# Four graph layers over 32 batches: score rows through a line in DRAM, statistics for pairs of batches, and work moved between VectorE, ScalarE and GpSimd

## The chip, the core and the metric

The kernel runs on one core of a Trainium2 chip. The metric is the device time of one execution in microseconds; a median over several executions is given. A profile of one execution shows, for each engine, every instruction with its start and end: PE (TensorE matmul, with PEld for its weight loads), DVE (VectorE), ACT (ScalarE), POOL (GpSimd) and SP (SyncE, which issues the DMAs here). Each engine works off its instructions in the order in which they stand in its own queue, and waits at an instruction whose inputs are not there yet.

## What is computed

The input x has 32 batches of 512 nodes with 128 features, in float32; adj is one 512 x 512 matrix of zeros and ones for all batches. Four layers follow one another, each in the frame `x = layernorm(x + layer(x))`, where the outer layernorm has no weights:

```python
# layer 0
e = (x @ a_i)[:, :, None] + (x @ a_j)[:, None, :]
mean, var = over all of e of one batch
e = leaky((e - mean) * rsqrt(var + 1e-14) * adj + adj)
h = sigmoid(einsum('bij,bjd->bid', softmax(e, axis=1), x))
# layer 1: h = x @ Wp + bp; masked softmax over leaky(s_src + s_dst), times adj, @ h
h_gat = relu(layernorm(..., gat_g, gat_b))
z = ((1 + eps) * h_gat + adj @ h_gat) @ W1 + b1
z = relu(layernorm(z, mlp_g, mlp_b))
h = relu(z @ W2 + b2 + h_gat)
# layer 2: A is a softmax over masked values; M the unit matrix
h = (A * M) @ (x @ W[0]) + (A * (1 - M)) @ (x @ W[1]) + bias
# layer 3: h = x @ W; masked softmax over leaky(e_src + e_dst), @ h, then elu
```

In layers 1 and 3 a score is the sum of one number of the row's node and one of the column's node. The column's numbers must therefore stand as a row of 512 on every partition.

## The kernel before

A batch is a tile of 128 partitions by 4 blocks by 128 features: node 128c + p is row p of block c. Constants (masks, the transposed adjacency, the matrix of layer 2, weights) are made once by `prepare_l1`, `prepare_l2` and `prepare_l3`. Then a loop over the batches (L1046) calls `layer0` to `layer3`. These functions do not issue anything: a recorder (L267) notes every operation, with what it reads and writes. At the end `order` (L335) gives them out one by one. Which of the operations that are ready comes next is read from a packed string, ORDER, which holds a complete order for all engines, worked out ahead; many batches are in flight at once. While it gives them out, `order` assigns tiles to 70 buffers of 128 x 512 in SBUF, to 110 small ones, and to the 8 PSUM banks, and where its own clock shows a gap on PE of over 250 ns and a bank is free, it puts transposes named `warm` into it (`fill`, L381). All operations are issued by one helper line, L418, so the profile is read by tile names.

Names end in the layer: `_r` layer 0, `_g` layer 1, `_t` layer 2, `_a` layer 3. A name with `p_` in front lies in a PSUM bank.

- `layer0` (L843). For the first five batches (FIRST) PE makes the two scores n of every node; from then on DVE does, with eight multiply-and-sum operations (xa_r). `rows_of` turns the scores into a row. The mean and the variance over all pairs come from two products with the matrix `share` (p_m_r, p_v_r) and tiny operations on DVE; two powers on POOL give r and its inverse sd. The three wide passes over e_r (DVE once, ACT twice) follow for each of four blocks, then the product p_o_r. After tanh on ACT, POOL makes y = 0.5 y + 0.5 and adds x, and DVE normalises (x_r).
- `rows_of` (L807) spreads a column over the partitions with four transposes on PE into a bank.
- `masked_softmax` (L817), for layers 1 and 3: the row from `rows_of` (p_d_g, p_d_a); four DVE operations add the mask and take the maximum (e_g, e_a, mx); two ACT passes follow.
- `layer1` (L916). After the product p_o_g the normalisation of hg has, in turn: four DVE operations with mean and reciprocal deviation, two POOL passes with gat_g and gat_b, a relu on DVE, and a POOL pass for hb. The product p_g_g needs hg.
- `layer2` (L975). POOL multiplies x by the diagonal of A (xd_t); PE transposes that; ACT copies it to dt_t.
- `layer3` (L1000). After the product p_o_a, elu is made of two ACT passes (ex_a), one POOL pass (exp - 1) and a DVE operation with the maximum; the result is normalised on ACT (x_a) and stored.
- `layer_norm` (L781) makes the statistics on DVE (st, mv), adds epsilon on POOL (ve, L761), takes the power -1/2 on POOL (rs, L756), and normalises on ACT with `normalise` (L766, which first makes sh on DVE) or on DVE with `normalise_dve` (L775).

Of the kernel before, what the change touches and what calls it, by code (L numbers as in the profile page):

```python
# [17 lines left out]
P = 128  # L18
# [10 lines left out]
WARM = 12  # L29
SMALLS = 110  # L30
BUFFERS = 70

# [4 lines left out]
c-mch$C4~Nk{tqCYY{55>b_>TaWRWA<AVSHXFRyGV`gPkiV%Rq{RkkeWLmI;bM_K?QzE{n5dRk9KSGH3FFb_T|N6&0<M%(m-yivVck;aapU+#_!`So7-  # L37
u1Biz6rq}e{c5rkoS|WL>{6}LXPVogpq5lMe-VVKF{ks|M%zld_LFvkgvlVHsrY`yYM)BIEB1a6er_!9&<T1`>zXUf1~rQ&|)uJ4>L^4B<ZR}P%#RbGm
&kr|CMA`L&^VYwuScJ%eLPBPiy~o;(utPx7H3)njRxhJ91B>m)@*wX*D~oZMMc3bKH+)V%-n(cU!qBrO3>a*smCzv)nl+9p~9`#strm1?HlQ(cuivCBn
Ed&IE%8ezC0KC}tfyjOnI4EaY(7&baWLMQV?O(UcC0hcWwazuB8;xCz`l9G3~vQETn?HW6&9CLSMk@H&JLXUO%TwuY;YY^wLVMX#wbS{JVmg*MZ81ZRk  # L40
phpZAudaaZqhnHDcX|*xZsG#NkuZeb2DXqN1nUqr`JEE;}C7Gesk<%fvm!j5WywKWUH&s(wvNwUVR-+cqA9NPpL~qd2WR%21c&mgF*+l7O5XK|~${81p
G9E$m*_enYzLj1Jt%y*<W#MXaQn=_<_Qa;_j4rX~8a&3Vq!>*K)&=94(YRy|7)X7TRJ5iVA3K8HyiGdWR8qqjn^tSDwINves^iK&c%K`drI}b-)uE(Zb
swSWqN@+B#<tU=9MzQJO>j9Fl6pkM6NVONurX)tTFbetoYQD0a<Cy0kJj)hWrNR_uIX_aQ|Hc<T&SUe(%M;FCOk+Pihi)mTn!;)DP18@AJNqnKhfjy^>
?_Q>pHG<o#|Ls&np~9IgS)&upxzJ9a=fklnC<*O1k8Pkf8+;N+3oQpMy)ux9oZ;Bp~9+5r<48hV1myIUwUKMzLWV(+D|-q#qk@bE`|7;^g7BTq~=LRwB
qAc@2e|*c!fc+=zga@|2U)xs)tK5Q0mM6yZunB2X7@cgOMMdEwlnlmzp5I))7o4k_a#+s(;;YXa$Ft+zF!Iz~pUi$CqD7jlJ1ry09B<IE;oaL^PP(bGC
3Ls3{=pl*<_s7os7K_yXwa!yea#33D>;=}^C2t|ny)HbTy;&;WVD~v{*SX#z4=ZbTFNUDy=BoWjTdbsW+ZNd73CX1ZJ6~iuMrvJ8EnO)mjX%r;VntR1O
7n~V^y1;k1mXbnCMr_3BAa1A{?7z=J2)-eeBdKyZIGV_ggXDaqL<3@^38koCbpT0}IMj}=;u6gjl!*;Os3}U3Vh8@vx8uOR1{uaQGY3@^#g8hc65)`V>
BCuJqKX(p0~nAP3`LzZ@(7GlWr0<PvS#B6>OLyvQZZ>`XVpy<v^oP10XeAdY*3ZxvkpiSr<i3{3kwk4<Bs4M>iq@=l(%!$C0T$@(x;U1d-<CS9MA=<rH
7ABw3I{w)@YS<#Q5bpOD1M<1dAdbo{DN6<$yn5bTp`Uqmw5k+6;s!mLiHKBwk!*E%TDZky#cjBCM>k7)h<U0UW9lJK$N!mIdErlT*)3G^UDDP4P-tudG
#~kThL%LAVlJ9|92;2f|1*DTE{v@W(v|X)r`JBKa_EET|x7)uoqOR4lRO*khF?c!V5r8-SG#tV%$RTx3xxqwS1EMp3~`0OMG|pfVqL<URuayhDN>M-1#  # L50
hNtx`yQN~8V5}?gEolFwCg5{62TZZN_!b!q8Gg2pIKs1#VXofdkdL-0^%p;OKm5955KZi`6Bq?Sg3Byp6MEuiv%2S!;R#@jMGY<5mcW;`~RjRD<3g~?z
%A?f0=Sb=pl0{<5!vWz5N>3y6l-1rI-05Q%Y?Uku;71_H@}P1&QXyG}ERk<f){>|W#4A*-l|Hh}vpGUn3Alr#QOE{?05Dum;+#}CiNe)*FRj>LqQt4Ux
Gn`V876E(81j+Z6uu?jU5yC4Te)-7Z66dv0**zRrId6yyb?_oAZv#%K!s79AYzYL%;vF5kI0V@($NCrk=fM{YCC+jeu8g$26YFEOgLnem(*aOx=wSNse
P#?HT{?10n}OhB;6iy36a5qPc}o5AYFs%wSmwC5~y3>dXB{wzy_-L2-q|Tr-_bZydp|k@4|F|Uhsj7GE%_%oM9AX{82MFbu)R*l)AkSu9hgBNi0C+;=r
~Q>~-|(%tt?u74lelfE!XxzD!gOU#*G^;!$hKRqrTo8U1}Oyb>rXA9L(}qnxX#q1HGN&9qQ;8q9IFr<In^79)D)bm*ho1QJf*63~n>Dk%^{G!8nW#+nN
RKt^^HaIb`nE6Jh(I*K{&dFBE3&38TP{UlP`Pfe?wrNxoYQBv<+v2idG7gCZ$LOfb>^*PUp3*R6c%b#2cPwpamgQq@^-C!lsX50&X@*mGTprZcZSTl-8
KL8=@@D0V*MLRl(uV#)A`^qZBgmxt(oltjPM<5T-G&Wv2uLfjzOu36l+Cj}BZ8^XahXNHxD<hEB{^iqJW%8(lUh$y=KVlvo+|!CLWtFOW%4?lzt%P?K@
O9>tECwt!H3K=jeUn4Zcvr!r#kqb5ca;l?c49QIk`bsf0_wi>|4B1k7i9yVAdy&76)BB?dWAB{+!xXVk*-?kh~SqH!;CGmw#tHd4iHE&f$dQ(NKcTf=M
a+MBA`GxEJ(;625JvG7;UAp!!Bhy(6njCi_V9}lhxr^v!z*hf?kdeb%#zs1D2wh>R=AGb)hW8q%Ozc$euapxLO-(&W6(~bEC{2*)M*o`+lGMycYi`Y}U
Fy55M30WAFR>8vA4IHJ*?87&Gjrf6V(_<~grxjQO2rj8FglUVZ$m@$K(9pV3DhSKWG!hEBpusUeWMmmxk?PsZH`*_p99L!2c}5h03u9T+2%Gh(Ijjm<(  # L60
YGt+gM(>r_B3s7^~u)u4vdw<l*b~%~MbR$r5c({Rp&n~xjfta1GbvHm!6)ngFreOe*OKnB9Qozd)3tlD3s*F(kZkLag2tBACAPG?jZ{Zk}t%s+mheXn$
&?{hp<N=@nCl+KO9xZm&BKQF1KQQ8Z+;QbLD?gqGc+tmwU!ueAiQ0NSZ?OJ*!d{KDw_4;WX9-ZR;g9?R_kOheY3;YY?FJ&;?K0-a9HyZNU-H6ff}7ae8
oSoL$XWxM@n&oR$#+m^p2se4&N4uf6;|Eh*ly{Os09OCb2x_*inhZTY6r8b)r6@X{sC&0JNql7yA;%nY#?yrC<Rx-KCnb=?L`n|`eX^Af!F{nxuJ>$E1
~pbDhwB8A!Y{7;oyIWsV!;+Ly_x_l5g-NEF!*8h)7_7S~10DJUJW*P|da!>$bZY)SYxWxnCAk7_$J7^AX<XGzG8-9C`DFcHZD;IprF0U9%V2HY$P2Ax<
SQ!Edb<>OMn*G%5kn&nl&U<S8r^eZuP&&rZe#MTkpZ_^!-y)>YB~^yu735rxOd1Lzf)kr&%M;SyR_y#uy;>OA3sTIiC($s$KX6&x$CG|C`AUZiV_oEOR
y-=Z|=U})0tO|?=9KcWkX?jtTphx`0M5XndWo|jT5lovX<WE(@ErrBqVTlDf?=X;UwIr+?Z%Rk3+V&ouiCZO&*$F2`3OxuhVz9Rz)Y_*{}(M&<~+X`0Z
I)r1%HUvjq3e-kU21dF}a8jYDn=Tfh<fdbx`p1TV|9LmZIb=OA(9CrrnQwtQxhkr+C79wgXX-V9qI+*=sShH5qEFyPY%cth$0<py5Y@*z96UZ_C(?zH_
ZoyfYx#HhYg{v~eqR{Kue!KA`GR%WB_PCFWi3cqkp&1rAnQ`$weK#eCM&8_RyMRBJ_FKaXN^?>1nFH9*X|9<7N+x)z=ZP_=W&9J$u_V<HA*_^bdal&gA
`Q?l(WhNnl(3Q!WqGqiD2X+N-RTF=g5(z{!$A+Nk8O7bXfzKFi2W2jk6k}mP-Y0gD%`y1XzaNK}H6Wwn0x|l@pH`&K}@!OBgX+S75`(PB0E>5}U*%fKt
>y8FP)N_s7yO=}FzP{fTRoyh;H$=Eiz~J`(xe`^^r_UuVZbAPASCw?L8w@TLnA>ptfVIeV^t&V^?fseAAnR7Hc@Vc73FZrFd)Yrp$J#zDG)HXSg$yby?  # L70
(Edv5;+v$)QZ;P>ucMK!6b2vQreA3vcJy9os1q*$+=al%lIPa6uMtfs)cnXXuI8X8kb`yfEctHVMC+pJPRG@j&kKV|h#PZ<{J_L69$B%i96VUc7)X6ws
kkwAw2RS?5z48BS_w~oU?&I9guNmg&*$VVr?~V={3jK9~nDSM(bF!=h%<;>7|G$SB0)=p}&Yn5hpo5|PNcUYbf6dWB09n96?g@|>9)CJWaB>t{C^itYG
;Z^Jz!Ea31Gv6J>{$;uKA`TN|BBl?!rqyHLMeelt7iwh5AS~#56sVQq@5hGJAB~ej0pxEF5MD9pCL>X29dCZG>A_{YJr|^r>uzqz8$Kcnr<L0Y1di9(B
k^oEdf_Ukc!sm;15H|ApyF<9uOe|>SOp_-o6F{T}LlEDBA_xH_KmpB1K<g6Tx@U7nv73(h;X{_4H}E82pHIS*sX~PoA?v{ta(tKsMpm1f^WF*nph^w7c
zlViCz<{>~b@WlkCqFpBt5{F|?!NVE%Rcn-ffL~h_#$Z7}Nwb>JqbZDek&@`$0g6v-<qYz53xo+E?&)qybnj+_4nkW!X4Mqlfa0~-p*@i)t40E~*K28K
3tOw4;$&lO_T_K?9Aw5%6eJ4VLD1}~t>_#`{p3VS2<qV<iPt=HrGYEJm*a^sxHb<W3bAFx^nOLre-ruu-<~yEo-SI={OAm5h(_WAQKi{u0+!%I#2!Jcx
YmjsN?DHa(&+~I0_q;hnDG%U=+nYI!&wb{Ms?FKP+Q(StdY<dO9`>9!Fc8Y(kr%zrvx;`ovRa<}f;TwE%|K%q75s$MBwc3J73|w~6h&l~=vDwWQ^==nh
b`p1B*GG*;LX7+LY7K^qN#uiq4$F09K{R%<PZvYq1g76=2i}V&yhMf92z6dj&9?xXiSt7kTA%5>LtQ(P>t0VXEV_?!3IF#Y>}f8@CwzaasKG2MUgo}$y
S}B5Da;44t{f3XlbPIEYKk>o4TsqGS1Ak8v^|<%ioGDo)_#@>x?FPuz_I!C@4-`aZfJ!d{hIeI26G9OmYPPRF@Y<VjZha3Xz-Ip-{yYsy+Av3bUjwbl?
m^t_+eHYR?3hOf4BT7fVpdTd=CBiF4y%9vouCcOSZ78n~VqTq1*xjWR&+So2q1MQ<gPtTfi6atyo$WUhxr&$ys!LAF*9eVT;cAOoQVNl@aBZWPfZ3@=p  # L80
6>cB~CuD>&RZ}`wB1p0djBE|1P-u`_aPcD$;Q=!6dpslCmbmYG0MXmn`@2>ZLgS$^xubh`f1z6NWl4#fF3O6M*rfWc;x{a}?3uQ{7#>wl<%e00MBoe-6
i#!$uVd!z7t~P+C6CqiZbja@5a|7u>dBUt^ZK0_$)$y=;vr(b0c$bsQo)+hePe?f!_z-N;Fi;9KTmDXdNw)oEWEHt#)-rn(=PVYLnFj_u!<{6s_O{+pK
tXQNAvhgVc1Sje4l7a-fNd6)i&R>QVewQt3#$R_jC)=;XN4+}22TmDme3Y?vdsY<T>~(*3KQPzUJ{9090RFqCLrrpbDShoMHJi9S!6UKdyPCXPFOo(X%
`M19zJr}yh|UhjI7Xah#MFxr2Z--_w8Ql=J89D76bJGLbwWZLBvw4Xwi$NL|fh4l)SFSYNNfzSYenl*kb?HttF-3J%_PU#^?o-9(HbpDEB&4L#Lh|+iG
$FA<xqd;FhC6Wy-c`%eq=AD6AcN2iN8xiaT-v7>s`RX(wuWD>aW|vp@@<@L^=zxQT^f_-Ii2uTsdy8*rM}MeoT!o%RAwa2wnM1h)#Q50}Z^lAH4)X^iW
b^T7X}XRPu`@i@tK9E+&6g0)a+Q};;}X;Y8B=d?Xe>r-+`TSg!+f$R;f&`@4`&i>BPh{oCrt=R<QnO!qA$sRbtb1{elPF@_zUbYgOD4uv;<DF(pvXjjF
`~0!L?)TTa^XKQseE#|V`SWQ%?@#>+>mA<(5fk6{`>y!}95QBKZRx*@c2<~)yd8Tv3Z6k}u{9>D7`_#B6(uMu^dLI8`>f+A92)&-=OMY6lmLKLVI%=*&
2!U5m!674*HA~<XqGxgD<B0n=b*|U%N-94pS|)>CImU;7fHt$$3W9+L)Q-ic@JstZDod5x`lMil53bLC_epn)et_2*uGb>K*oMMeP5jiGXk$&6+L*z;o
d_*UIhFy;A)Voa7;KEf%Zm5L!X?)IZ_=6Cz=kd;bSjrW($+KJx<n+=>RF@kvPDRy<&;t<0|DUA$}%^gqhy)14h+`=9vY0(uHWXwoFm!f;0pdL87$1bh;
cu(?DYDqLj^Te>ZU7aKDfb@19ILYx+QJeg3?k@B3n)KYs<%d#~xgt3N-__cF_>HQRb;Q{z)VD1#@``!4>T<@@ztK0Z$T^UwXSoBjFc&+jk&JRJ-Vp?f`  # L90
-JKMY`?O+;%Arq%;V)BOIHhqr@7H)91ohK<zS;gX8w#?{H4j;Eg%9Zc4Tx*ZZYCcWKuL04A-3pkqt<_QJ&UM!qWQuD|K;#0%;kjUWih~ORSHS}mQ6XH#
1kD$Tbc}nJq6#{yfUiL-dKH(r<2&=yu5X2HeB*W;*C-X4OhyGYBd2?hP&%EE6se2J?RAm@4?rAPDjMdBl}1Z#lubUv&{}_Hj9<g}(LEzpLI#3lAOg@Ln
WX5fkVhHRT!0)!L28b+=P^JG$pzp!NQ9Smu`}@#vK_kPh~c=9=|}Q|gm{q9_AE9a8RvEh!yN_^A*Cjw-pFhL;V_hO=k3wpKJlH~)6?L(1M1Nh9-DXYD1
# [53 lines left out]
class V:  # L147
# [11 lines left out]
    def rearrange(self, pattern, **k):  # L159
# [4 lines left out]
        if "(" in left:  # L164
            idx = self.idx.reshape(1, n, -1)
            if right.split()[1] != left.split("(")[1].split()[0]:
                idx = idx.transpose(0, 2, 1)
        else:
            idx = self.idx.reshape(1, -1)
# [46 lines left out]
def cost(engine, op, args, k):  # L216

    n = max((v.n for v in views(args, k)), default=1)
    if op == "dma_start":
        return 470, 0  # L220
# [859 lines left out]
```

## Time and profile before

| what | value |
|---|---|
| median of three executions | 1060.61 us (1060.21 to 1060.83) |
| the profiled execution | 1060.28 us |
| its span from first to last instruction | 1058.6 us |
| instructions | 22,953 |
| mean granted clock of TensorE | 0.988 |
| DMA over the span | 20.21 MB, mean 19 GB/s |
| p_o_a, p_o_r, p_o_g on PE | 1024 records each, busy 141.8, 129.3, 132.0 us |
| p_t_a from e_a, p_t_g from e_g on PE | 512 records each, busy 77.6, 74.3 us |
| p_d_a, p_d_g on PE (the rows of scores) | 128 records each, busy 21.4, 20.1 us |
| e_a, e_g on DVE | 128 each, busy 82.2, 81.8 us |
| hg_g on POOL, with gat_g and with gat_b | 32 each, busy 41.8, 41.2 us |

In a line of a group stand the line of the kernel, the engine, the operation, what is written and what is read, the count, the busy time and the mean length of one, and the idle time of the engine just before such an instruction with what ended it. In a list of waits stand who waited for whom, the total in us, how often, and the longest. Records of one engine may overlap, so a busy time is not the sum of the lengths. A wait of an engine that is not the bound need not cost anything.

### The profile page before, as it was taken

To read this page: it belongs to the slowest core of one execution; us is meant where nothing else is said; L and a number is where in the kernel's file an instruction comes from. 1 tells how busy PE (TensorE), PEld (TensorE's weight loads), DVE (VectorE), ACT (ScalarE), POOL (GpSimd) and SP (SyncE) were. 2 spreads that over 40 slices of the span, in tenths; PEclk is the share of its full clock that TensorE was granted. 3 is DMA by queue.
4 is the path that set the end of the run, shared out by engine and by line. 5 is a ranking of instruction groups with operands and counts; after the bars stand their busy time and mean duration, and the time that the engine had idled before them with its cause. 6 is when DMAs were issued, how large, how long until landed. Compare 5 with 4: busy or idle time off the path is not lost.

```text
span 1058.6 us, 22953 instructions
## 1 busy us (share of the span) xinstructions
PE 1027.1 (97%) x7464; PEld 880.6 (83%) x7464; DVE 953.1 (90%) x4291; ACT 911.8 (86%) x2128; POOL 620.2 (59%) x777
## 2 busy tenths in 40 slices
PE   8999999999999999999999999999899999999994
PEld 8868987886889798988879879797888888888884
DVE  6899999899998899999999998889989889879975
ACT  5469855779999899969899989889998899989997
POOL 6647764656565655485665655566466664563642
PEclk9999999999999999999999999999899999999997
DMA  7000000000000000010100000001000000000012
GB/s 194 11 2 1 2 1 2 1 2 1 2 1 21 21 22 1 22 29 14 41 1 22 21 2 21 22 21 41 1 14 9 21 21 2 21 11 2 11 41 70
DMA packets 38199, 20.21 MB, mean 19 GB/s; under 512 B 3136, under 2 KB 37568, under 8 KB 38080
## 3 DMA queue, kind: packets, MB, share of 16 engines
q1 hardware_dynamic: 37792, 18.23, 6.5%
q8 instruction: 59, 0.97, 0.4%
q10 hardware_dynamic: 288, 0.52, 0.2%
q14 instruction: 60, 0.49, 0.1%
HBM read 10.36 MB, written 8.39 MB: 18 GB/s over the span
## 4 chain that ended last, share of the span: by engine, by line
PE 64%; DVE 27%; ACT 3%; POOL 3%; issue 2%; DMA 0%; POOLq 0%; ACTq 0%; DVEq 0%
PE p_o_r L418 8%; PE p_g_g L418 8%; PE p_o_g L418 8%; PE p_y_t L418 7%; PE p_o_a L418 7%; PE p_t_g L418 5%; PE p_t_a L418 4%; PE p_o_t L418 4%; DVE e_r L418 3%; DVE e_a L418 3%; DVE e_g L418 2%; DVE nm_g L418 2%; PE p_h_g L418 2%; PE p_z_g L418 2%; PE p_h_a L418 2%; DVE xa_r L418 2%
## 5 line engine op out<-in xcount | busy, mean ns | idle before, releaser
L418 PE MATMUL p_o_a<-h_a,nm_a 128*128 128x128 f32 x1024 | 141.8, 278 | 3.2 <-DVE nm_a L418 3.2
L418 PEld LDWEIGHTS p_o_a<-h_a,nm_a 128*128 128x128 f32 x1024 | 128.9, 194 | 7.5 <-issue 3.7
L418 PE MATMUL p_o_r<-xs_r,e_r 128*128 128x128 f32 x1024 | 129.3, 282 | 4.7 <-POOL xs_r L418 4.6
L418 PE MATMUL p_o_g<-h_g,nm_g 128*128 128x128 f32 x1024 | 132.0, 276 | 1.6 <-DVE nm_g L418 1.6
L418 PEld LDWEIGHTS p_o_r<-xs_r,e_r 128*128 128x128 f32 x1024 | 123.8, 197 | 9.0 <-POOL xs_r L418 7.0
L418 PEld LDWEIGHTS p_o_g<-h_g,nm_g 128*128 128x128 f32 x1024 | 123.5, 192 | 6.9 <-issue 4.6
L418 PE MATMUL p_g_g<-a1t,hg_g 128*128 128x512 f32 x256 | 121.3, 598 | 1.4 <-DVE hg_g L418 1.2
L418 PE MATMUL p_y_t<-l_rest_t,x_g 128*128 128x512 f32 x256 | 122.1, 595 | 0.0
L418 ACT ACTIVATE e_g<-e_g,sd_g 128x512 f32<-128x512 f32 x128 | 83.6, 720 | 15.8 <-DVE mx_g L418 15.8
L418 ACT ACTIVATE e_a<-e_a,sd_a 128x512 f32<-128x512 f32 x128 | 87.3, 730 | 9.3 <-DVE mx_a L418 9.3
L418 ACT ACTIVATE e_g<-e_g,nmx_g 128x512 f32<-128x512 f32 x128 | 91.2, 719 | 3.5 <-DVE sd_g L418 1.9
L418 DVE TENSOR_TENSOR nm_g<-p_t_g,adj_t 128x512 f32<-128x512 f32 x128 | 83.0, 678 | 11.8 <-PE p_t_g L418 11.7
L418 ACT ACTIVATE e_a<-e_a,nmx_a 128x512 f32<-128x512 f32 x128 | 91.8, 729 | 1.1 <-DVE nmx_a L418 1.0
L418 ACT ACTIVATE e_r<-e_r,r_r 128x512 f32<-128x512 f32 x128 | 91.2, 716 | 1.1
L418 DVE SCALAR_TENSOR_TENSOR e_r<-p_s_r,tb_r,adj_t 128x512 f32<-128x512 f32 x128 | 89.1, 738 | 2.9 <-PE p_s_r L418 2.9
L418 ACT ACTIVATE e_r<-e_r 128x512 f32<-128x512 f32 x128 | 76.8, 625 | 15.4 <-DVE e_r L418 14.9
L418 DVE CUSTOM_DVE_ANT_0 e_a<-p_d_a,mask 128x512 f32<-128x512 f32 x128 | 82.2, 678 | 7.7 <-PE p_d_a L418 7.7
L418 DVE CUSTOM_DVE_ANT_0 e_g<-p_d_g,mask 128x512 f32<-128x512 f32 x128 | 81.8, 680 | 3.4 <-PE p_d_g L418 3.4
L418 PE MATMUL p_t_a<-ident,e_a 128*128 128x128 f32 x512 | 77.6, 273 | 0.0
L418 PE MATMUL p_t_g<-ident,e_g 128*128 128x128 f32 x512 | 74.3, 274 | 0.0
L418 PEld LDWEIGHTS p_g_g<-a1t,hg_g 128*128 128x128 f32 x256 | 43.9, 190 | 34.6 <-issue 31.8
L418 ACT COPY nm_a<-p_t_a 128x512 f32<-128x512 f32 x116 | 65.6, 589 | 7.7 <-PE p_t_a L418 7.5
(206 smaller groups left out, 2960.1 us busy)
## 6 DMA issues: line engine op xcount, KB each, us to landing
x_in<-in_x SPq DMA_DIRECT2D x32, 256.0 KB, 3.2
out<-x_a SPq DMA_DIRECT2D x32, 256.0 KB, 2.4
adj_n<-in_adj ACTq DMA_DIRECT2D x2, 256.0 KB, 3.9
adj_n<-in_adj SPq DMA_DIRECT2D x2, 256.0 KB, 5.3
w<-in_L_gnn_W SPq DMA_DIRECT2D x3, 64.0 KB, 3.1
a_ij<-in_L_gnn_a SPq DMA_DIRECT2D x1, 128.0 KB, 4.0
b_bc<-in_L_gnn_b SPq DMA_DIRECT2D x2, 64.0 KB, 4.1
l_w<-in_L_gnn_W SPq DMA_DIRECT2D x2, 64.0 KB, 3.3
```

What stands on the lines that cost most here:

```text
L418: f(*[real(a) for a in args], **{n: real(a) for n, a in k.items()})
```

## The change

The tiles, the layers and their results stay the same. Ten things move:

1. Rows of scores of layers 1 and 3 go by DMA for batches 5 to 29: a column of 4 numbers per partition is written to a line of 512 numbers in DRAM (twelve lines take turns), and that line is read back, broadcast to 128 partitions, into an SBUF buffer. Other batches keep the transposes.
2. From batch 5 on, the mean and the variance of layer 0 are made for two batches at once, in tiles twice as wide.
3. sd of layer 0 is a product on DVE (var times r) in place of a second power on POOL.
4. y of layer 0 is one DVE operation, 0.5 y + x; the added constant 0.5 is left out, which the normalisation after it takes away in any case. x_r is normalised on ACT.
5. epsilon is added on DVE (ve), and nrz of layer 3 is made there.
6. hg of layer 1 is made by two DVE operations for each block, with gat_g and gat_b in them; the relu goes to POOL.
7. In layer 2 xd falls away: x itself is transposed, and DVE multiplies by the diagonal as a row (l2_drow, made once) while it takes dt out of the bank.
8. exp - 1 of layer 3 is made on ACT, apart from the last four batches.
9. In the last four batches xt, h and x_a of layer 3 are made on DVE in place of ACT.
10. ORDER is a new string for these operations.

```diff
+GROUP = 2
+LATE = 4
+ROWS_FROM = 5
+ROWS_LATE = 2
+LINES = 12
...
+        drow = const([P, N], "l2_drow")
+        R.act.copy(drow, rows_of(diag, "o_t"))
...
     def rstd_of(mv, name):
-        R.pool.tensor_scalar(ve, mv[:, :, 1], LN_EPS, None, ALU.add)
+        R.dve.tensor_scalar(ve, mv[:, :, 1], LN_EPS, None, ALU.add)
...
-    def rows_of(col, name):
+    def rows_of(col, name, by_dma=False):
+        if by_dma:
+            t = Tl(lines, "line" + name)
+            R.sp.dma_start(V(t, (("rearrange", ("o (c p) -> p (o c)",), {"p": P}),)), col)
+            pr = buffer(name)
+            R.sp.dma_start(pr, V(t, (("__getitem__", (0,), {}), ("partition_broadcast", (P,), {}))))
+            return pr
         pr = bank(name)
...
+    def statistics0(xs, bs):
+        G = len(bs)
...
-        R.pe.matmul(pm[:, 0 : 2 * NB], share, n, start=True, stop=True)
+        R.pe.matmul(pm[:, 0 : 2 * G * NB], share, n, start=True, stop=True)
...
-        R.pool.tensor_tensor(sd, var, phalf, ALU.pow)
+        R.dve.tensor_tensor(sd, var, r, ALU.mult)
...
-        R.pool.tensor_scalar(y, y, 0.5, 0.5, ALU.mult, ALU.add)
-        R.pool.tensor_tensor(y, y, xb, ALU.add)
+        R.dve.scalar_tensor_tensor(y, y, 0.5, xb, ALU.mult, ALU.add)
         x1 = node_tile("x_r")
-        layer_norm(x1, y, "_r", False)
+        layer_norm(x1, y, "_r", True)
...
-        e, z = masked_softmax(sd, C["mask1"], "_g")
+        e, z = masked_softmax(sd, C["mask1"], "_g", ROWS_FROM <= b < B - ROWS_LATE)
...
-        normalise_dve(hg, o, mv, rsqrt(ve, "_go"))
-        add_bc(hg, hg, C["gat_g"], R.pool, ALU.mult)
-        add_bc(hg, hg, C["gat_b"], R.pool)
-        R.dve.tensor_scalar(hg, hg, 0.0, None, ALU.max)
+        for c in range(NB):
+            R.dve.scalar_tensor_tensor(hg[:, c, :], o[:, c, :], mv[:, c, 0:1], C["gat_g"], ALU.subtract, ALU.mult)
+        r = rsqrt(ve, "_go")
+        for c in range(NB):
+            R.dve.scalar_tensor_tensor(hg[:, c, :], hg[:, c, :], r[:, c : c + 1], C["gat_b"], ALU.mult, ALU.add)
+        R.pool.tensor_scalar(hg, hg, 0.0, None, ALU.max)
...
-        R.pool.tensor_tensor(xd, xb, C["l2_diag"].unsqueeze(2).to_broadcast([P, NB, D]), ALU.mult)
+        xd = xb
...
-        R.act.copy(dt, pd)
+        R.dve.tensor_tensor(dt, pd, C["l2_drow"], ALU.mult)
...
-        xt = transposed(xb, "_a", R.act.copy)
+        xt = transposed(xb, "_a", R.dve.tensor_copy if b >= B - LATE else R.act.copy)
...
-        R.pool.tensor_scalar(nrz, rz, -1.0, None, ALU.mult)
+        R.dve.tensor_scalar(nrz, rz, -1.0, None, ALU.mult)
...
-        R.pool.tensor_scalar(ex, ex, 1.0, -1.0, ALU.mult, ALU.add)
+        if not (b >= B - LATE):
+            R.act.activation(ex, ex, AF.Copy, bias=-1.0)
+        else:
+            R.pool.tensor_scalar(ex, ex, 1.0, -1.0, ALU.mult, ALU.add)
...
-        layer_norm(x4, y, "_a")
+        layer_norm(x4, y, "_a", not (b >= B - LATE))
```

The h of layer 3 changes in the same way as xt. The write and the read of a row stand in SP's queue, where the loads of x and the stores of the result stand too; SP holds the read until its write has landed.

## The prediction

> **What bounds the kernel now.** I read the busy shares first, then the span cut into a start, a middle and an end.
>
> ```profile
> PE 1027.1 (97%) x7464; PEld 880.6 (83%) x7464; DVE 953.1 (90%) x4291; ACT 911.8 (86%) x2128; POOL 620.2 (59%) x777
> ```
> ```profile
> 0.00:100.00 100.00, 94.02 (x635) 80.47 (x636) 84.61 (x332) 62.39 (x136) 61.31 (x82) 0.98 0.22 55
> 100.00:1030.00 930.00, 920.94 (x6739) 788.43 (x6738) 851.26 (x3888) 827.27 (x1938) 550.27 (x683) 1.00 0.05 14
> 1030.00:1058.60 28.60, 12.14 (x94) 11.71 (x91) 17.19 (x72) 22.16 (x58) 8.63 (x14) 0.75 0.26 74
> ```
>
> The columns of the windows are PE, PEld, DVE, ACT, POOL, clock, DMA. PE is busy 99% of the middle, but its records overlap, so I count its work by spacing, from the chain of waits in order of time:
>
> ```profile
> 995.67 3.44 PE p_y_t L418 x8
> ...
> 999.54 0.87 PE p_t_a L418 x8
> 1000.64 1.79 PE p_o_t L418 x16
> ```
>
> A 512-column record takes 3.44/8 = 0.430 us, a transpose 0.109, a 128-column record of a product 0.112 (a product leaves two records). The middle has 500 wide records (tiles p_g_g 244, p_y_t 256), so its PE work is 500 x 0.430 + some 1,800 transposes x 0.109 + 4,440 x 0.112 = 908 us at most (a few records are shorter), some 97% of 930. PE is the bound; DVE at 851 (91.5%) and ACT at 827 (89%) follow closely. That closeness is the main thing: a saving on PE is worth only the distance to the next engine.
>
> DVE operations overlap too. What one takes from DVE is the distance between starts in the timeline:
>
> ```profile
> 604.82 1.36 DVE L418 TENSOR_SCALAR hg_g<-p_o_g,mv_go,rs_go 128x128 f32<-128x128 f32 x4 [0.19 <-POOL rs_go L418]
> ...
> 610.37 1.13 DVE L418 SCALAR_TENSOR_TENSOR y_a<-p_o_a,rz_a,ex_a 128x128 f32<-128x128 f32 x4 [3.56 <-POOL ex_a L418]
> ...
> 614.24 1.11 DVE L418 TENSOR_SCALAR x_r<-y_r,mv_r,rs_r 128x128 f32<-128x128 f32 x4
> ```
>
> Take the last one off each run of four (0.40, 0.34, 0.34 long) and divide by three: hg 0.32, y_a 0.263, x_r 0.257. A 512-wide operation takes 0.605 (three e_g start at 620.48, 621.09 and 621.71 us); the relu on hg 0.30, a 256-wide copy 0.34, and a 4-wide one about 0.075 by the same view.
>
> **The change, engine by engine.**
>
> PE loses 200 transposes (rows for 25 batches, two layers, four each): 200 x 0.109 = 21.9 us. Paired statistics take 26 products off p_m_r and p_v_r, 52 records x 0.112 = 5.8. Four transposes for l2_drow come in at the start, 0.4. PE work in the middle falls by about 27, to 881.
>
> DVE loses x_r (128 x 0.257 = 32.9), the old hg (128 x 0.32 = 41.0), the relu (32 x 0.30 = 9.6) and 43 tiny operations (3.2): 86.7. It gains two operations per block for hg (256 x 0.263 = 67.3; the second has all inputs in SBUF, taken like y_a), y_r (32 x 0.605 = 19.4), dt (19.4), 243 tiny ones (ve 160, nrz 32, sh_r 32, sd_r 19: 18.2), and in the last four batches copies and normalisations from ACT (4 x 0.605 + 8 x 0.34 + 16 x 0.257 = 9.2): 133.5. Net **+47 us**, total near 1,000. About 10 of it lies in the start and the end, so the middle holds 851 + 37 = 888.
>
> ACT gains x_r (128 x 0.43, the row of x_t, 55.0) and ex in 28 batches (0.65 each, 18.2), loses dt (18.7) and late work (16 x 0.43 + 8 x 0.363 + 4 x 0.583 = 12.1): +42, to 954; middle about 869.
>
> POOL loses hg (83.0), y_r (62.0), xd (33.4), ve (40.8), sd_r (18.0), ex (17.5), nrz (9.1) and some r_r (5.4), and gains the relu (32 x 0.625 = 20): 620 becomes 371. None of it was the bound, but DVE waited for it:
>
> ```profile
> DVE y_a L418 <- POOL ex_a L418: 14.6, 9, 5.4
> DVE nm_g L418 <- PE p_t_g L418: 11.7, 12, 3.1
> DVE st_r L418 <- POOL y_r L418: 10.0, 8, 3.4
> ```
>
> The first and third go, apart from four batches of ex. The chain from hg to p_g_g loses two POOL passes of 1.3 us, and that from x_g to p_d_t one of 1.04. What is late next is DVE's own queue.
>
> **The row trip** is the new wait. The write (512 elements of 4 bytes into a line) waits on SP for sd on DVE; the read, broadcast to 128 partitions, waits on SP for the write; the first e operation waits on DVE for the read. Behind it stands everything later on DVE; behind the read on SP stand other rows, x_in and out. Nearest rows (KB, us to landing):
>
> ```profile
> x_in<-in_x SPq DMA_DIRECT2D x32, 256.0 KB, 3.2
> out<-x_a SPq DMA_DIRECT2D x32, 256.0 KB, 2.4
> ...
> a_col<-in_L_gnn_a SPq DMA_DIRECT2D x1, 1.0 KB, 4.7
> ...
> l_eps<-in_L_gnn_eps SPq DMA_DIRECT2D x1, 0.5 KB, 3.3
> ```
>
> Read: 3.2. Write: 2.4 (out) to 4.7 (a_col at the crowded start); I take 3.3. Trip 5.6 to 7.9, taken 6.5. The changed kernel's instruction order shows the cover: between the last sd of a batch and the first e operation that needs its row stand 25 to 176 DVE operations, by the spacings above 6.0 to 41.7 us of work, median 9.6. Only two trips of 50 have less than 6.5, and lack 0.8 us together. At 8 us 15 lack 9.6; at 9, 23 lack 28; at 10, 29 lack 54. So I take 1 us, with 0 and 10 as ends. The late change of the last two batches keeps PE rows, so no trip stands in the final chain. Two rules of the Trainium skill speak against my choice:
>
> - "DMA: Bandwidth & Descriptors", Specifications: a piece under 512 B makes the DMA engine read, modify and write. No row here stores 4-byte pieces to DRAM; l_eps and a_col only load them. If this doubles the write (estimate, 2 x 3.3), the trip is 9.8 and DVE loses about 48 us instead of 1. I go by the rows, since 4-byte loads do not stand out.
> - "SBUF — State Buffer", Who interferes with whom: a DVE operation with two SBUF inputs and a GpSimd operation that reads SBUF exclude one another for the whole instruction. The rows move from PSUM to SBUF, so 200 e operations fall under it. By the rule each meets a running POOL operation with chance 371/1058 = 0.35 and waits half of one (0.5 us): 35 us. The trace:
>
> ```profile
> L418 DVE TENSOR_SCALAR x_r<-y_r,mv_r,rs_r x128: 304/340/1370, 37.0 to 956.5; 128x128 f32<-128x128 f32 x128
> L418 DVE SCALAR_TENSOR_TENSOR y_g<-y_g,x_r x32: 655/680/897, 108.3 to 1006.1; 128x512 f32<-128x512 f32 x32
> L418 DVE TENSOR_TENSOR y_t<-p_o_t,xbias_t x32: 653/678/692, 131.7 to 1019.5; 128x512 f32<-128x512 f32 x32
> ```
>
> The maxima (897, 1370) show that the lock exists, but y_g with two SBUF inputs has mean 683 against 675 of y_t: 8 ns, 200 x 0.008 = 1.6 us; by x_r, whose mean is 381 against a median of 340, it is 8. I take 5, and set it against what x_r itself loses in such waits (128 x 41 ns = 5), which goes with it.
>
> **The sum.** PE 881, DVE 888, ACT 869 in the middle: the bound passes from PE to DVE and is only 20 us lower than the 908 of PE. PE reached 97% with the others at 91.5 and 89; now three engines stand within 20 us, which costs freedom, against less POOL in the chains and 200 fewer bank fillings. I take 96.5%: 888/0.965 = 920, 10 less than 930. The end saves about 2 (for four batches ACT, at 22 of 28.6 the busiest there, gives work to DVE). Span 1058.6 - 12 = 1046.6; with the 1.7 between span (1058.6) and profiled time (1060.28), **1048 us**, 1.2% under it. The median of 1060.61 is 0.3 away.
>
> **Rivals.**
> - *PE's whole saving comes through* (DVE packs to 98.5%: 888/0.985 = 901.5, 28 less, end 2): 1030. For it: DVE was busy 98.9% between 550 and 600 us. Against: ACT and PE would need 96 and 98% at once.
> - *The saving drowns*: DVE at 95.5% needs 930, the old middle; with port waits either way, 1055 to 1064, middle 1059. For it: 79 us of the old middle were DVE idle while PE was already full.
> - *The trip outlasts its cover*: DVE stalls at the first e_g or e_a. It decides from about 8.5 us per trip, where the loss (18) outgrows the gain (12); at 9 us 1048 + 27 = 1075. A long gap on PE costs more than itself:
>
> ```profile
> 740.00:750.00 10.00, 7.28 (x55) 6.05 (x54) 10.00 (x43) 10.00 (x27) 4.43 (x6) 1.00 0.00 0
> 750.00:760.00 10.00, 8.58 (x51) 8.58 (x52) 7.55 (x37) 7.43 (x19) 4.39 (x8) 0.66 0.01 2
> ```
>
>   After a gap of 4.1 us the granted clock is 0.66 in this window. Against it: most covers exceed 8 us.
> - That the change does not do what it says is excluded: the built order has the 100 row DMAs and 200 fewer transposes.
>
> **Chances.** Forecast (1038 to 1055) 0.42; whole saving 0.10; drowned 0.23; trip 0.25. A difference of 0.2%, some 2 us, is what can be told from none. Of the drowned case 0.04 is faster, 0.08 the same, 0.11 slower: faster 0.56, same 0.08, slower 0.36. The range from 1028 (just under the whole saving) to 1075 (a trip of 9 us) leaves out the longer trips and the luckiest packing; the likeliest case's own is 1038 to 1055.
>
> **What would show it.** Right: DVE busy near 1,000 and above 95% of the middle, PE with idle time for DVE, POOL near 370, waits of DVE for row DMAs below 5 us in all, a trip near 6.5. Wrong: DVE idle before e_g or e_a on a DMA for tens of us; e operations well above 0.69 us; DVE not above PE.

## The result, and the profile after

| | median, us | range |
|---|---|---|
| before, measured beside it | 1060.65 | 1060.21 to 1060.83 |
| after | 1263.52 | 1262.33 to 1266.73 |

The ratio is 1.1918 (1.1896 to 1.1941): 203 us slower, where 12 faster were forecast. First the busy shares of the page, then the span cut as before (columns: PE, PEld, DVE, ACT, POOL, clock, DMA):

```profile
PE 1071.3 (85%) x7212; PEld 903.7 (72%) x7212; DVE 1004.5 (80%) x4551; ACT 952.1 (75%) x2225; POOL 417.8 (33%) x383
```
```profile
100.00:1230.00 1130.00, 957.07 (x6453) 806.56 (x6453) 895.96 (x4117) 866.71 (x2030) 357.42 (x311) 0.92 0.13 22
1230.00:1261.40 31.40, 19.00 (x162) 17.76 (x160) 24.98 (x107) 22.32 (x58) 8.92 (x10) 0.86 0.29 84
```

No engine is full. DVE works 1004.5 us, ACT 952.1, close to the 1,000 and 954 of the prediction; but the middle has grown from 930 us to 1130, and DVE fills 79% of it where it filled 91.5%. PE has fewer instructions and a longer busy time: its granted clock in the middle is 0.92, it was 1.00 (experiment 6, in which the waits are gone, has 1.00 again). Of the 203 us of span, 51 are more work on DVE, about the 47 of the prediction, and 151 are more idle time of DVE: 257 us, where it had 106. Who waited for whom (total, times, longest):

```profile
DVE e_g L433 <- DMA d_g<-lined_g: 116.8, 22, 11.0
DVE e_a L433 <- DMA d_a<-lined_a: 70.6, 15, 10.0
DVE nm_g L433 <- PE p_t_g L433: 10.3, 11, 2.0
DVE xa_r L433 <- DMA x_in<-in_x: 7.6, 3, 3.8
```

DVE stands 187.4 us before rows, more than all that its idle time has grown by. The same view of SP's own queue, and the DMA part of the page (KB each, median us to landing), say which half of the trip is long:

```profile
SPq L433 <- DMA lined_g<-sd_g: 210.1, 24, 13.0
...
SPq L433 <- DMA lined_a<-sd_a: 172.8, 22, 11.6
```
```profile
d_g<-lined_g SPq DMA_DIRECT2D x25, 256.0 KB, 5.1
d_a<-lined_a SPq DMA_DIRECT2D x25, 256.0 KB, 5.3
...
lined_g<-sd_g SPq DMA_DIRECT2D x25, 2.0 KB, 12.5
lined_a<-sd_a SPq DMA_DIRECT2D x25, 2.0 KB, 10.3
```

By these medians a write of 2 KB takes 1.9 to 2.5 times as long as a read that moves 256 KB. And SP, which issues in order, stands 383 us at reads whose write is not done. One trip in the timeline, SP's rows and then DVE's:

```profile
582.00 0.36 SPq L433 DMA_DIRECT2D lined_a<-sd_a  x1
590.51 0.33 SPq L433 DMA_DIRECT2D d_a<-lined_a  x1
```
```profile
592.34 0.16 DVE L433 RECIPROCAL rz_r<-z_r 128x4 f32<-128x4 f32 x1
595.61 0.69 DVE L433 CUSTOM_DVE_ANT_0 e_a<-d_a,mask 128x512 f32<-128x512 f32 x1 [3.11 <-DMA d_a<-lined_a]
```

sd_a is done at about 581.97 (its two copies on DVE start at 581.75 and take 0.22 us). The write is issued at 582.00, the read can go at 590.51 (8.5 us), and the first e operation starts at 595.61 (5.1 us later): a trip of 13.6. DVE had 10.5 us of other work, a cover a little above the median of 9.6, and stood for 3.1. Put through the covers of the prediction, a trip of 14 us outlasts 44 of 50 and lacks 212 us in all; the 187 measured are of that size.

### The profile page after: what moved, and what is told of

Its sections match the earlier page's. It is cut to its first block, busy times and chain, and to the rows that moved or that the text cites. A ratio compares the mean times of both kernels' runs of the same rounds, so it can differ in the third digit from the quotient of the medians.

```text
span 1261.4 us, 22504 instructions
## 1 busy us (share of the span) xinstructions
PE 1071.3 (85%) x7212; PEld 903.7 (72%) x7212; DVE 1004.5 (80%) x4551; ACT 952.1 (75%) x2225; POOL 417.8 (33%) x383
## 4 chain that ended last, share of the span: by engine, by line
DVE 34%; DMA 27%; PE 25%; ACT 5%; issue 5%; POOL 3%; SPq 0%; POOLq 0%; ACTq 0%; DVEq 0%
DMA lined_g<-sd_g 8%; DMA d_g<-lined_g 6%; DMA d_a<-lined_a 6%; DMA lined_a<-sd_a 5%; PE p_o_r L433 4%; DVE e_g L433 4%; DVE e_a L433 3%; DVE nm_g L433 3%; PE p_o_g L433 3%; DVE hg_g L433 3%; PE p_g_g L433 3%; DVE e_r L433 2%; PE p_o_a L433 2%; PE p_t_g L433 2%; PE p_y_t L433 2%
## 5 line engine op out<-in xcount | busy, mean ns | idle before, releaser
L433 DVE CUSTOM_DVE_ANT_0 e_g<-d_g,mask 128x512 f32<-128x512 f32 x100 | 69.0, 719 | 116.8 <-DMA d_g<-lined_g 116.8
L433 PE MATMUL p_o_r<-xs_r,e_r 128*128 128x128 f32 x1024 | 146.3, 288 | 17.5 <-POOL xs_r L433 17.5
L433 PEld LDWEIGHTS p_o_r<-xs_r,e_r 128*128 128x128 f32 x1024 | 135.2, 203 | 24.4 <-POOL xs_r L433 19.9
L433 PE MATMUL p_o_a<-h_a,nm_a 128*128 128x128 f32 x1024 | 150.2, 284 | 0.2 <-DVE nm_a L433 0.2
L433 PEld LDWEIGHTS p_o_a<-h_a,nm_a 128*128 128x128 f32 x1024 | 136.0, 201 | 4.5 <-issue 2.7
L433 PE MATMUL p_o_g<-h_g,nm_g 128*128 128x128 f32 x1024 | 136.5, 281 | 1.0 <-DVE nm_g L433 1.0
L433 DVE CUSTOM_DVE_ANT_0 e_a<-d_a,mask 128x512 f32<-128x512 f32 x100 | 67.6, 690 | 70.6 <-DMA d_a<-lined_a 70.6
L433 PE MATMUL p_t_a<-ident,e_a 128*128 128x128 f32 x512 | 85.8, 286 | 10.2 <-DVE nm_g L433 7.6
L433 PE MATMUL p_t_g<-ident,e_g 128*128 128x128 f32 x512 | 81.7, 282 | 13.5 <-DVE nm_g L433 6.5
L433 DVE TENSOR_TENSOR nm_g<-p_t_g,adj_t 128x512 f32<-128x512 f32 x128 | 83.4, 679 | 10.6 <-PE p_t_g L433 10.3
L433 PEld LDWEIGHTS p_t_a<-ident,e_a 128*128 128x128 f32 x512 | 65.5, 149 | 19.8 <-DVE nm_g L433 7.8
## 6 DMA issues: line engine op xcount, KB each, us to landing
lined_g<-sd_g SPq DMA_DIRECT2D x25, 2.0 KB, 12.5
lined_a<-sd_a SPq DMA_DIRECT2D x25, 2.0 KB, 10.3
```

Source lines behind the costliest of these rows:

```text
L433: f(*[real(a) for a in args], **{n: real(a) for n, a in k.items()})
```

## The experiments

Theory after the result: the write is slow, and the rest of the change is as forecast. Rivals: the whole trip by DMA is slow on this queue; the new order, or the other edits, cost time too. Each kernel that is timed has its ratio to the kernel before, run on the same chip.

**1. The write by itself (m1_writes).** All layers are left out. Seven forms of write, each followed by the read of the line, so that from the issue of the write to the issue of the read is the write's time: as in the change, with 512 pieces of 4 bytes (scat; tight takes them from adjacent columns); 128 pieces of 16 bytes (join); 512 pieces of 4 bytes, each in 512 bytes of its own (apart); 128 adjacent pieces of 4 bytes (single); 128 pieces of 64 bytes (wide); 4 pieces of 512 bytes (fourrows).

```diff
-    nc.sync.dma_start(line.rearrange("o (c p) -> p (o c)", p=P), col[:, 0:4])
+    nc.sync.dma_start(line.rearrange("o (p c) -> p (o c)", p=P), col[:, 0:4])
...
+    far = line.rearrange("o (c p k) -> p (o c) k", p=P, k=128)[:, :, 0]
+    nc.sync.dma_start(far, col[:, 0:8].rearrange("p (c k) -> p c k", k=2)[:, :, 1])
```

> Leaves out all four layers: it copies one tile to the output and then makes row trips one after another, each write waiting for the read before it. Seven forms of write, four times each: scat (512 single numbers, as in the change), tight (the same with the four source numbers side by side), join (128 pieces of 16 bytes in the line), apart (512 single numbers, each in its own 512 bytes), single (128 single numbers), wide (128 pieces of 64 bytes), fourrows (4 pieces of 512 bytes). Theory 'pieces' (each small piece costs the DMA engines a fixed time): scat, tight and apart alike near 8.5 us from write to read as in the changed kernel; join, single and wide near 3.5 to 4; fourrows 2.5. Theory 'shared block' (small writes to the same 512 bytes wait for one another): apart near 3 although it has 512 pieces, scat and tight 8.5, join and single in between. Theory 'queue' (the write is short, and in the changed kernel it stands behind other transfers): all forms below 4 us here.

The timeline of SP, one pair of each of four forms (start us, length of the issue):

```profile
77.92 0.36 SPq L74 DMA_DIRECT2D line_scat<-col_scat  x1
87.34 0.33 SPq L91 DMA_DIRECT2D row<-line_scat  x1
...
98.92 0.32 SPq L78 DMA_DIRECT2D line_join<-col_join  x1
100.33 0.32 SPq L91 DMA_DIRECT2D row<-line_join  x1
...
130.77 0.37 SPq L81 DMA_DIRECT2D line_apart<-col_apart  x1
132.56 0.32 SPq L91 DMA_DIRECT2D row<-line_apart  x1
...
215.87 0.32 SPq L83 DMA_DIRECT2D line_single<-col_single  x1
223.38 0.32 SPq L89 DMA_DIRECT2D row<-line_single  x1
```

9.4, 1.4, 1.8 and 7.5 us; wide takes 1.4 and fourrows 1.2. The write is as slow alone as in the kernel, so the crowd on the queue is not the cause. None of the three theories holds as it stands: the one of the shared block is nearest, but join, which it puts in between, is fast. 512 pieces of 4 bytes are fast where they lie apart, so neither their number nor their size alone is. Slow are pieces of 4 bytes that lie side by side.

**2. How near is side by side (m2_spacing, m3_serial).** 128 pieces of 1 to 8 numbers at a distance of 1 to 128 numbers. In m2_spacing forms that do not depend on each other ran into one another, and their times cannot be told apart; m3_serial writes all into one block.

```diff
-line = hbm.tile([1, P * step], F32, name="line_" + name)
+line = block[:, 0 : P * step]
 nc.sync.dma_start(line.rearrange("o (p k) -> (o p) k", p=P)[:, 0:n], xt[:, 0:n])
```

> All four layers are left out: x is loaded, 32 plain stores of it go to the output, and then for each of 13 forms five writes of 128 pieces into a line of DRAM stand one behind the other, each held until the one before it is done, so the distance of two issues is the time of a write. The pieces have 1, 2, 4 or 8 numbers of 4 bytes and begin 1 to 128 numbers apart. Theory (pieces that fall into one block of DRAM wait for one another, each being read, changed and written back): a write of single numbers takes some 8 us at a distance of 1, and gets shorter by steps as the distance grows, down to under 2 us once a block holds one piece; a piece of 16 bytes, adjacent or not, should then be slow as well where the block is larger than 16 bytes. Rival (what counts is the size of the piece alone): single numbers take some 8 us at every distance, 16 bytes 1.4. Rival (alignment: a piece that does not fill and begin at a granule of 16 or 32 bytes is slow only while neighbours share the granule): slow at distances 1 and 2, perhaps 4, fast from 8 on, and 2 numbers at a distance of 2 in between.

> All four layers are left out. The 13 forms of the run before, but now all writes go into one block of DRAM, so that each of the 65 waits for the one before it and the time of each form stands alone. Each form has 128 pieces. Theory (pieces in one block wait for one another): single numbers take some 8 us at a distance of 1 and fall with the distance in steps; from the mixed run before, distances up to 16 numbers (64 bytes) may be slow, from 32 on fast. Rival (size of the piece alone): 8 us at every distance. For 2 and 4 adjacent numbers a piece, some 2 to 4 us and 1.4 to 2 us; for 8 numbers 1.4.

In m2_spacing forms at a distance up to 16 numbers landed in some 10 us and those from 32 on in 3, but several of them were under way at once. Alone (five writes each; the first 4-byte form has a first write of 10.9, left out):

| numbers a piece | distance | pieces in 32 bytes | us |
|---|---|---|---|
| 1 | 1 (4 bytes) | 8 | 7.3 to 8.9 |
| 1 | 2 | 4 | 3.3 to 4.1 |
| 1 | 4 | 2 | 1.4 to 2.0 |
| 1 | 8 and more, to 128 | 1 | 1.39 to 1.44 |
| 2 | 2 | 4 | 2.8 to 4.0 |
| 2 | 4 | 2 | 1.5 to 2.1 |
| 4 | 4 | 2 | 1.6 to 2.0 |
| 4 | 8 | 1 | 1.4 |
| 8 | 8 | 1 | 1.4 |

Three rows of its timeline for distances of 1, 2 and 8 (each pair is one write):

```profile
49.70 0.32 SPq L61 DMA_DIRECT2D block<-xt  x1
58.41 0.32 SPq L61 DMA_DIRECT2D block<-xt  x1
...
79.94 0.32 SPq L61 DMA_DIRECT2D block<-xt  x1
83.26 0.32 SPq L61 DMA_DIRECT2D block<-xt  x1
...
103.87 0.32 SPq L61 DMA_DIRECT2D block<-xt  x1
105.28 0.32 SPq L61 DMA_DIRECT2D block<-xt  x1
```

The time goes by how many pieces share 32 bytes of DRAM, whatever their size: the rival of the granule of 32 bytes in the expectation of m2_spacing came out, and the other two theories fell. A further piece costs the whole write 0.4 to 1 us ((8.4 - 1.4) / 7 = 1.0 with eight, (1.8 - 1.4) / 1 = 0.4 with two). That they wait for one another there is the plain reading; the runs show the time, not the wait itself.

**3. No wait for the rows (e1_other_row).** The rows still go to DRAM and back, but e reads another row that is always there, so e of batches 5 to 29 leaves the rows of scores out.

```diff
-            return pr
+            return Other(pr, C["l2_drow"])
```

> The changed kernel with its order untouched and all row DMAs still issued, but the e operations of layers 1 and 3 in batches 5 to 29 read the constant row l2_drow in place of the row from the line: the rows of scores are left out there. Nothing on DVE waits for a row. Theory 'trip' (the row comes later than its cover on DVE, the rest of the change is worth what the forecast's sum says): 1035 to 1060 us, and no DVE wait on a row DMA. Theory 'rest' (the moved work, port locks or the packing cost the time): over 1150 us.

1125.02 us, ratio 1.0618 (1.0598 to 1.0638): between the two, so both theories missed. Waits of DVE and of SP:

```profile
DVE xa_r L442 <- DMA x_in<-in_x: 57.8, 9, 15.1
```
```profile
SPq L442 <- DMA lined_g<-sd_g: 218.1, 23, 11.8
SPq L442 <- DMA lined_a<-sd_a: 199.3, 23, 12.5
```

The wait for rows is gone and a second one comes to light: SP still stands 417 us at reads, and the loads of x behind them come late. In the changed kernel only 7.6 us of that wait show; that DVE is so late there by itself is the plain reading, and it was not tested.

**4. No write (e4_no_write).** Order and reads as they are, but only the first row is written, and later reads fetch that line; so the rows of later batches are left out.

```diff
-            R.sp.dma_start(V(t, (("rearrange", ("o (c p) -> p (o c)",), {"p": P}),)), col)
+            R.sp.dma_start(V(t, (("rearrange", ("o (c p) -> p (o c)",), {"p": P}),)) if first else Unsent(t), col)
...
-            R.sp.dma_start(pr, V(t, (("__getitem__", (0,), {}), ("partition_broadcast", (P,), {}))))
+            R.sp.dma_start(pr, told if first else Other(told, real))
```

> The changed kernel in its own order of instructions, but only the first row is written to DRAM; the writes of all later rows of scores are left out, and every read fetches that one kept line again, 256 KB over 128 partitions, with every e operation waiting for its read as before. So rows of scores of later batches are left out. Theory (the slow write is the whole cause, through the trip and through SP, which stands at each read until the write before it is done): the trip is then the read alone, about 5 us, fewer than three of 50 covers are shorter, SP is not held, x_in comes in time: DVE about 1,000 us busy at 94 to 96% of the span, 1045 to 1062 us. Rival (the reads, which move 12.8 MB more, or the new order itself cost the time too): e_g, e_a or xa_r still wait for DMAs for tens of us, 1085 us or more.

1052.81 us, ratio 0.9925 (0.9908 to 0.9941). Its busy shares, and the first of DVE's waits:

```profile
PE 1007.6 (96%) x7212; PEld 854.7 (81%) x7212; DVE 1004.6 (96%) x4551; ACT 944.7 (90%) x2225; POOL 419.6 (40%) x383
```
```profile
DVE e_g L449 <- DMA d_g<-lined_g: 6.2, 1, 6.2
```

Without 49 writes of 2 KB the time is 1263.5 - 1052.8 = 211 us shorter, more than the whole loss. DVE has the same 1004.6 us of work; its idle time falls from 257 us to 46. The reads still move their 256 KB each, and neither they nor the rest of the change cost time that shows. But this run takes away more than the write: a read of the kept line needs no new scores, so SP's waits for sd_g and sd_a before the writes (75.0 and 84.9 us in the changed kernel) are all but gone too, and many reads are issued before their scores exist. Experiment 6 keeps that dependence.

**5. Fast writes, first way (e2_pieces16).** The scores lie by kind, a partition writes its four numbers as 16 bytes, and the line holds node 128c + q at place 4q + c; e reads the row in steps of 16 bytes.

```diff
-V(t, (("rearrange", ("o (c p) -> p (o c)",), {"p": P}),)), col
+V(t, (("rearrange", ("o (p c) -> p (o c)",), {"p": P}),)), col
...
-                e[c], pd, mask[:, c, :], 1.0, LOWEST, ALU.add, ALU.max, mx[:, c : c + 1]
+                cut(e[c], "p (c q) -> p c q"), cut(pd, "p (q c) -> p c q"), cut(mask[:, c, :], "p (c q) -> p c q"),
+                1.0, LOWEST, ALU.add, ALU.max, mx[:, c : c + 1]
```

> The changed kernel with its order untouched; sd lies by kind, so the column to be sent is 16 bytes in one piece per partition, the line takes it in 128 pieces of 16 bytes in place of 512 of 4, and the e operations read the row in steps of 16 bytes. Theory 'pieces': the time from write to read falls from 8.5 us to about 4, the trip from 14 to about 9, and by the list of covers the lack falls from 212 us at 14 to 28 at 9: 1070 to 1100 us. Theory 'queue' (SP's order or traffic makes the write late, not its pieces): stays at 1240 to 1265 us. If the stepped read slowed the e operations, their mean would rise above 0.72 us.

1136.92 us, ratio 1.0724 (1.069 to 1.0758). The writes are done in 1.4 us, and no wait for a row is left. But (min/median/max of e, and the busy shares):

```profile
L433 DVE CUSTOM_DVE_ANT_0 e_g<-d_g,mask x100: 1051/1101/2072, 179.3 to 947.3; 128x512 f32<-128x512 f32 x100
```
```profile
PE 1034.1 (91%) x7212; PEld 865.1 (77%) x7212; DVE 1087.9 (96%) x4551; ACT 954.2 (84%) x2225; POOL 430.1 (38%) x383
```

A row read in steps of 16 bytes makes e 1.10 us long in place of 0.687: 200 x 0.41 = 83 us more on DVE, and the time is 84 above experiment 4. "SBUF — State Buffer" of the Trainium skill, Door 1: The DMA port swizzle, says that SBUF is read by lines of 16 bytes and that an access which goes to a new line pays; this row agrees and gives the price. (The step comes with an access in four runs of 128; the two were not parted.)

**6. Fast writes, second way (e6_dealt).** Now masks and e lie in the line's order too, so DVE reads straight on; the step of 16 bytes moves to the PE transposes of e.

```diff
-                R.pe.transpose(pt[:, blk(c)], e[c][:, blk(j)], ident)
+                R.pe.transpose(pt[:, blk(c)], dealt(e[c], j), ident)
...
-            R.pool.tensor_scalar(mask1[:, c, :], edges[c], -FILL, FILL, ALU.mult, ALU.add)
+            R.pool.tensor_scalar(dealt(mask1[:, c, :]), by_block(edges[c]), -FILL, FILL, ALU.mult, ALU.add)
```

> The changed kernel in its own order of instructions, with the whole computation. The scores of a batch lie by kind, so that a row is written in 128 pieces of 16 bytes, and the line keeps the nodes in the order in which they come, 4q+c for node 128c+q. The row is read contiguously, masks and e stand in that order, and only the PE transposes of e read it in steps of 16 bytes (rows that PE makes are written in such steps). Theory (adjacent 4-byte pieces make the write slow, and the step of 16 bytes made e slow): a write takes 1.4 us, a trip about 6, no DVE wait for rows beyond 5 us in all, e stays at 0.68 us, DVE about 1,000 us busy: 1045 to 1062 us. Rival (PE pays for the step as DVE did): transposes from e at 0.2 us or more in place of 0.11, 800 x 0.1 = 80 us more on PE, which is at 1,030 already: 1110 us or more.

1052.59 us, ratio 0.9916 (0.9902 to 0.9931). It computes everything, and it takes 0.8% less time than the kernel before and 17% less than the changed one. Busy shares, SP's waits, and the group of transposes from e_a:

```profile
PE 1016.4 (97%) x7212; PEld 869.0 (83%) x7212; DVE 1007.1 (96%) x4551; ACT 945.4 (90%) x2225; POOL 421.6 (40%) x383
```
```profile
SPq L433 <- DMA lined_g<-sd_g: 32.1, 22, 3.0
...
SPq L433 <- DMA lined_a<-sd_a: 28.8, 20, 3.6
```
```profile
L433 PE MATMUL p_t_a<-ident,e_a 128*128 128x128 f32 x512 | 85.4, 283 | 0.0
```

SP stands 61 us in place of 383, and e has a median of 0.684 us. A transpose takes 283 ns on PE, against 274 in experiment 4. The step shows in the weight loads that go with the transposes, first in the changed kernel (shortest, median and longest in ns), then here (busy us, mean ns):

```profile
L433 PEld LDWEIGHTS p_t_a<-ident,e_a x512: 138/142/233, 159.1 to 1244.4; 128*128 128x128 f32 x171
```
```profile
L433 PEld LDWEIGHTS p_t_a<-ident,e_a 128*128 128x128 f32 x512 | 74.0, 205 | 7.8 <-issue 6.0
```

A load takes some 63 ns longer, 1024 times. The loads run beside the products and PEld is busy for 83% of the span, so this costs nothing here that shows. The rival fell.

**7. Rows on PE, the rest of the change (e3_rows_on_PE).** All batches keep the transposes, in an order made for that.

```diff
-        if by_dma:
+        if False:
```

> All of the change but the row trip: rows of layers 1 and 3 by four transposes on PE in every batch, all other parts as changed, in an order that follows the changed one as closely as the transposes and the banks allow. Theory 'trip': 1035 to 1060 us, with PE back near 1,025 us of busy time. Theory 'rest': over 1100 us.

1057.27 us, ratio 0.9973 (0.996 to 0.9985):

```profile
PE 1027.1 (97%) x7411; PEld 877.6 (83%) x7411; DVE 1001.6 (95%) x4551; ACT 945.3 (89%) x2225; POOL 408.9 (39%) x383
```

The other nine edits are worth some 3 us, and the rows by DMA, once their writes are fast, 4.7 more. The order is another one here, so the split is rough.

**8. A longer cover in place of a shorter trip (e7_long_cover, e8_order_short).** First the changed kernel with its slow writes in an order worked out for them (only the ORDER string differs), then the same order with the layout of experiment 6.

```diff
-ORDER = """
...
+ORDER = """
...
```

> The changed kernel with its 4-byte writes, the whole computation and every operation as it is, only in another order (a new ORDER string), worked out for a write of 12.5 us and a read of 6 us in place of the short ones. Theory (the trip itself does no harm, the order gave it too little cover): writes stay at 8 to 11 us, waits of DVE for rows and for x_in fall below 30 us in all, 1055 to 1085 us. Rival (SP stands some 400 us at the reads, and no order can keep x_in and the rows in time behind it): DVE still waits 60 us or more for DMAs, 1110 us or more.

> The whole computation. The order of the run with long cover (1126.6 us), and the layout dealt by node, whose writes take 1.4 us in place of 8 to 11; nothing else differs from the run with long cover. Theory (that order is worse in itself: to begin the trips earlier it pulls work apart elsewhere): the time falls little, 1095 to 1125 us, DVE waits for rows near 0, and the rest of its idle time stays. Rival (the trip still costs 60 us there in spite of the cover, through small waits that shift everything behind them): 1050 to 1075 us, DVE at 95% of the span.

1126.58 us, ratio 1.063 (1.0606 to 1.0653), and 1092.4 us, ratio 1.0299 (1.0272 to 1.0327). The waits for rows with the slow write:

```profile
DVE e_a L431 <- DMA d_a<-lined_a: 16.7, 4, 5.9
...
DVE e_g L431 <- DMA d_g<-lined_g: 7.5, 5, 3.6
```

187.4 us of waits become 24.2, and DVE does not wait for x, as the theory had it; but the time is the rival's. SP still stands 202 us at reads. The second run parts the rest. 1126.6 - 1092.4 = 34 us are still the slow write's. 1092.4 - 1052.6 = 40 us are this order's own, with DVE at 94% where experiment 6 has 96. Both expectations for the second run missed, by 3 us and by 17. Whether a better order could hide the slow trip for nothing was not found out.

## Why the prediction was wrong

**The step that failed** is the size of one term: "Write: 2.4 (out) to 4.7 (a_col at the crowded start); I take 3.3", and with it "Trip 5.6 to 7.9, taken 6.5" and "So I take 1 us, with 0 and 10 as ends". The write takes 8.5 us in the trip shown, 9.3 to 11.1 alone, 10.3 and 12.5 in the page's medians; the read takes 5.1 in place of 3.2, and the trip is 14 or more. The table in the prediction, which has 9.6 us lost at 8, 28 at 9 and 54 at 10, was going the right way and stopped too early: at 14 it is 212. The four rows that bounded the write are loads, or stores in pieces of 512 bytes. None stores small pieces side by side. The prediction says so itself, and yet took their spread for the bounds of the unknown; an operation without a near row needs a bound from something that resembles it in the respect that matters, or a range left open upwards.

**The mechanism was named** as the third rival, with its place (DVE at the first e_g or e_a) and the point from which it decides (8.5 us). It was given 0.25 and a trip of 9. Two slips in the sums change nothing: by the prediction's own table a trip of about 8.1 us already eats the gain of 12, and 908 us of PE are 97.6% of 930.

**The rule set aside.** By "DMA: Bandwidth & Descriptors" of the Trainium skill, Specifications, pieces under 512 bytes are read, modified and written; at twice the write the prediction worked out 48 us lost. The rule was nearer to the truth than the rows, but neither of them gives 203. The size of a piece does not decide here: 4 bytes in 512 of their own take 1.8 us with 512 pieces, and 16 bytes 1.4. What decides is how many pieces meet in 32 bytes.

**What no step priced:** SP. The prediction names what stands behind the read on SP and gives it no cost. Experiment 3 shows it: 58 us of waiting for x once DVE no longer waits for the rows. Its time is 72 us above experiment 4 (1125.0 - 1052.8); that the rest of the 72 comes from SP too is not shown, since experiment 4 also leaves the writes out and lets reads go early.

**What held.** DVE's work (1,000 forecast, 1004.5), ACT's (954, 952.1), the bound passing from PE to DVE, and the 5 us for the port between DVE and GpSimd, against the 35 of its second rule. The e operations with a row from SBUF, in the changed kernel (mean ns behind the busy time), and one of them in the timeline:

```profile
L433 DVE CUSTOM_DVE_ANT_0 e_g<-d_g,mask 128x512 f32<-128x512 f32 x100 | 69.0, 719 | 116.8 <-DMA d_g<-lined_g 116.8
L433 DVE CUSTOM_DVE_ANT_0 e_a<-d_a,mask 128x512 f32<-128x512 f32 x100 | 67.6, 690 | 70.6 <-DMA d_a<-lined_a 70.6
```
```profile
586.30 1.54 DVE L433 CUSTOM_DVE_ANT_0 e_a<-d_a,mask 128x512 f32<-128x512 f32 x1
```

With the row in PSUM their means were 680 and 678 ns in the kernel before, so 200 of them lose 100 x 0.039 + 100 x 0.012 = 5 us; the medians (687 and 682 against 681) hide it, because a few long ones make it up. The one shown starts while POOL works on hb_g (from 586.02 for 1.27 us) and is 0.86 us longer than the usual 0.68, which fits a wait for the end of that pass; the prediction's maxima alone do not show a lock.

With the write out of the way the time is 1052.8 or 1052.6, inside the forecast's own 1038 to 1055, in part by luck: its terms are less good than their sum. In experiment 6:

```profile
100.00:1020.00 920.00, 902.36 (x6472) 770.34 (x6471) 900.38 (x4128) 863.58 (x2037) 361.34 (x314) 1.00 0.12 27
1020.00:1050.40 30.40, 18.24 (x155) 17.30 (x153) 24.02 (x105) 21.35 (x56) 8.05 (x10) 0.89 0.30 87
```

DVE works 900 us in the middle, not 888, and fills 97.9% of it, not 96.5: the two errors cancel at the 920 forecast. The rest is 30.4 us where 26.6 were forecast, the whole difference between 1048 and 1052. The cut at 1020 is chosen so that the middle has the 920 us of the forecast, so how the 900 and the 30.4 part the work depends on it, and only the sum is measured. The filling does not depend on it: with a cut at 1010 it is 97.8%.

**POOL** came out at 417.8 against 371. The relu was taken at 0.625 us from other one-input passes of the same shape; its median is 1.496 and its 32 passes are busy 50.9 us in place of 20: 31 of the 47 us. POOL has room, so it costs little: with fast writes PE waits 11.4 us for it.

## What to carry to other kernels

A transfer that takes the place of work on an engine is to be priced by its slowest leg, and a write of small pieces to DRAM by how many of them share 32 bytes, not by its bytes: let each partition write at least 16 bytes together, and take the new order up where it costs nothing: here in the masks, which are made once, and in weight loads, which had room, not in an operation of the busiest engine that runs 200 times. A wait in a queue that issues in order can cost twice, once for the one who waits for the data (187 us here) and once for what stands behind it (58 us for x when the first wait is gone). Covers are fitted to one trip time, so ask what the sum is at twice that time before trusting it.

## What the runs showed of the hardware that was not expected

- 512 pieces of 4 bytes side by side in DRAM take 9.3 to 11.1 us to write, 128 of them 7.3 to 8.9 (and 10.9 once, the first); with one piece per 32 bytes 128 take 1.4.
- The e operation of DVE with its row read in steps of 16 bytes: 1.10 us against 0.687. PE transposes with such an input: 283 ns against 274, and their weight loads 205 ns against 142.
- A maximum with 0 on GpSimd over 128x512 takes 1.50 us (median of hg_g), a multiply and add of the same shape 0.62 (ex_a).
